# A block's row maxima, split before or after they are transposed: four 32x32 transposes on VectorE instead of one on TensorE with a rounding on ScalarE

## The chip, the cores and the metric

One core of a Trainium2 chip runs the whole kernel. The metric is the time of one execution on the device in microseconds (us). Five engines work side by side, each through its own list of instructions in order: TensorE (PE in the profile, with its weight loads as PEld), VectorE (DVE), ScalarE (ACT), GpSimd (POOL), and SyncE (SP), which here only issues the transfers (DMAs). An instruction waits on semaphores for what it needs from others, and everything behind it on its engine waits with it.

## The reference

Eight sequences of 1024 tokens with 256 features go through an attention layer with rotary positions (16 heads of 16, four shared key heads) and then a layer with ternary weights; each layer has a normalization before it, one behind it, and the residual added.

```python
q = x @ Wq; k = x @ Wk; v = x @ Wv            # x: layernorm of (8, 1024, 256)
k = jnp.repeat(k.reshape(B, S, Hkv, hd), G, axis=2)   # H = 16, Hkv = 4, G = 4, hd = 16
v = jnp.repeat(v.reshape(B, S, Hkv, hd), G, axis=2)
q = _rope(q, ...); k = _rope(k, ...)
scores = jnp.einsum('bhqd,bhkd->bhqk', q, k) / jnp.sqrt(jnp.float32(D))   # D = 256
p = jax.nn.softmax(scores, axis=-1)
o = jnp.einsum('bhqk,bhkd->bhqd', p, v)
...
x = x + _layernorm(o.reshape(B, S, D) @ Wo)
x = x + _layernorm(jnp.einsum('bsd,od->bso', _layernorm(x), ternary(weight) * alpha) + bias)
```

The part that matters here is the softmax: before the exponential, each row of scores has its largest score subtracted.

## The kernel before, in words

The work is cut into 16 units of 512 queries (half a sequence each), and a unit into 4 blocks, so there are 64 blocks. A block holds four heads of 512 queries (in the last unit: all sixteen heads of 128 queries), against the 1024 keys of its sequence. Queries and keys lie stacked in `q_st` and `k_st` with 64 rows for a head: three bands of 16 rows hold the high and low parts of the numbers (so that products in the rounded type `F32R` come out nearly exact), and rows 48 and 49 (`NROW`) are kept for the maxima: the keys have -1 there, and the queries first 0 and later the high and the low part of the query's maximum. One product then gives the score less its maximum.

So each block is gone through twice. In the first pass (`max_scores`, L583 to L619) TensorE forms the scores with queries on partitions, two half rows of 512 keys to a tile `sm` in PSUM (L600), of which there are two, and VectorE reduces each tile to its maxima in `mx` (`reduce_halves`, L625): either both halves in one instruction of 128x1024, or one half at a time (128x512), as the order has it. In the second pass (`exp_one`) TensorE forms the scores with keys on partitions in a tile `se` (L673), of which there are three, each one bank of PSUM; ScalarE takes the exponential (L694) into `e`, and TensorE multiplies by the values (`av_piece`, L714). The first pass runs 40 to 52 of these score tiles ahead of the second; a block has 32 of them.

The order on TensorE, VectorE and ScalarE is written out by hand. The loop goes by **windows** (`window`, L1164): for each of 3 score tiles (or 2) it records one `se` product with its exponential and one half row of maxima, and behind them the products with the values of the window before last. Other work that needs a bank of PSUM for itself (projections, transposes, the output layers of units before and after; `banked`, L1093) takes its bank from the three of `se`. Where such a piece of work stands ready, the window has 2 score tiles, and one piece is done in the bank that is left (`window_size`, L1105; `do_parts`, L1127). GpSimd and SyncE are ordered by the scheduler of the framework.

The change is in what happens once a block's maxima are complete:

- `shift_join` (L638) reduces the two half rows to one maximum on VectorE and writes it twice, for the high and the low part: `mc`, 128x32 from 128x64 (L642). The queries are still on partitions.
- Some steps later (`due`, L619; `collect`, L1122) `shift_rows` (L644) is put at the head of the ready work. It is `banked`: a window of 2 tiles carries it. TensorE transposes `mc` into `pm`, 32x128 in PSUM (L648), and ScalarE rounds `pm` to `F32R` into `mh` (L650).
- In the next window, `shift_low` (L653, called by `take_low`, L1140) lets VectorE compute `ml` = `mh` * `low` + `pm` (L657), where `low` is a column with -1 on the rows of the low part and 0 on the others, made at the start (L525 to L528). Rows of the high part then hold the rounded maximum, the others what rounding left. Two DMAs of SyncE (L664) write the 32 rows into rows 48 and 49 of `q_st`.

The block's first exponential product waits for these two DMAs; `behind_shift` and `behind_latest` (L1017, L1022) place some other DMAs behind them in SyncE's list.

Of the kernel before, what the change touches and what calls it, by code (L numbers as in the profile page):

```python
# [8 lines left out]
F32 = mybir.dt.float32  # L9
F32R = mybir.dt.float32r  # L10
AF = mybir.ActivationFunctionType
ALU = mybir.AluOpType
AX = mybir.AxisListType
# [3 lines left out]
P = 128  # L17
# [4 lines left out]
UT = 4  # L22
# [6 lines left out]
def kernel(  # L29
# [29 lines left out]
    nc = tc.nc  # L59
# [13 lines left out]
    const = ctx.enter_context(tc.tile_pool(name="const", bufs=1))  # L73
    xp = ctx.enter_context(tc.tile_pool(name="xp", bufs=2))
    small = ctx.enter_context(tc.tile_pool(name="small", bufs=4))
# [107 lines left out]
    def psum(shape, name, dtype=F32):  # L183
        if spare[0]:
            spare[0] += 1
            if spare[0] % 5 < 2:
                return ps_mx.tile(shape, dtype, tag="sm", name=name)
        return ps_e.tile(shape, dtype, tag="se", name=name)
# [314 lines left out]
    def row_pickers():  # L503

        sel = q_st[1].rearrange("p j c t -> p (j c t)")[:, : 4 * G * P]
        nc.vector.memset(sel.bitcast(F32), 0.0)
        sel = sel.rearrange("p (l e j x) -> p l e j x", l=2, e=2, j=G)
        selk = tailp.tile([P, 2, P], F32R, tag="hl1", name="selk")
        nc.vector.memset(selk.bitcast(F32), 0.0)
        half = small.tile([P, P // 2], F32, tag="half", name="half", bufs=1)  # L510
        nc.vector.tensor_tensor(half, ident[:, : P // 2], ident[:, P // 2 :], ALU.add)
        eye = half.rearrange("p (a j d) -> p j a d", a=2, j=G)
        for e in range(2):
            for band, l in enumerate((0, 1, 0)):
                rows = sel[:, l, e].rearrange("p j (a b d e) -> p j a b d e", a=2, e=2, d=HD // 2)
                nc.vector.tensor_copy(rows[:, :, :, band, :, e], eye)
        eye = ident.rearrange("p (l r a d) -> p l r a d", l=2, r=2, a=2)
        for band, l in enumerate((0, 0, 1)):
            rows = selk.rearrange("p r (a b d) -> p r a b d", a=2, d=HD)
            nc.vector.tensor_copy(rows[:, :, :, band, :], eye[:, l])  # L520
        shift = const.tile([P, 1], F32, name="shift")
        rows = ident.rearrange("p (a d) -> p a d", a=2)[:, :, NROW:]
        nc.vector.tensor_reduce(shift, rows, AX.XY, ALU.add)
        nc.vector.tensor_scalar(shift, shift, -1.0, None, ALU.mult)
        low = const.tile([8 * UT, 1], F32, name="low")  # L525
        rows = ident[: 8 * UT, : 8 * UT].rearrange("p (a l x) -> p a l x", a=2, l=2)[:, :, 1]
        nc.vector.tensor_reduce(low, rows, AX.XY, ALU.add)
        nc.vector.tensor_scalar(low, low, -1.0, None, ALU.mult)  # L528
        return sel, selk, shift, low

    class PickRows:

# [38 lines left out]
    mx = {}  # L571
# [11 lines left out]
    def max_scores(v):  # L583


        i, k = divmod(v // 2, 2 * NK)
        u, part = i // G, v % 2
        if i == 0:
            a, ch, t, r2 = 1 - part, k // NK, k // 2 % UT, k % 2
        else:  # L590
            a, ch, t, r2 = 1 - k % 2, part, k // 4, k // 2 % 2
        queries = block_queries(i, r2)
        queries = queries[:, t * P : (t + 1) * P] if u < NU - 1 else queries[:, t]
        if part == 0:
            sm[0] = ps_mx.tile([P, 2, 512], F32, tag="sm", name=f"sm_{i}_{k}")
            if k == 0:
                mx[i] = small.tile([P, 2, 2 * UT, 2], F32, tag="mx", name=f"mx_{i}")
            reduced.clear()
        rows = slice(64 * a, 64 * a + 64)
        scores = nc.tensor.matmul(  # L600
            sm[0][:, part, :],
            queries[rows],
            k_st[(u // UPB) % 3][rows, r2, ch * 512 : (ch + 1) * 512],
            start=True,
            stop=True,
        )
        if part == 0:
            return
        if reduced:
            tc.declare_no_dep(scores.ins, early[0], reason="another bank")  # L610
        if i == 0:
            nc.vector.tensor_reduce(
                mx[i][:, ::-1, head_and_tile(i, r2, t), ch], sm[0], AX.X, ALU.max
            )
        else:
            reduce_halves(i, k, 2)
        if k == 2 * NK - 1:
            shift_join(i)
            due.append((v // 4 + (1 if i < 3 else 2), i))  # L619

    def reduce_halves(i, k, n):

# [10 lines left out]
        if i > 0 and v % 2:  # L633
            reduce_halves(i, k, 1)

    sm, mhl, shifts, reduced, early = {}, {}, {}, [], [None]

    def shift_join(i):  # L638

        m = mhl[i] = small.tile([P, 2, 2, 2 * UT], F32, tag="mc", name=f"mc_{i}")  # L640
        halves = mx.pop(i).unsqueeze(2).to_broadcast([P, 2, 2, 2 * UT, 2])
        nc.vector.tensor_reduce(m, halves, AX.X, ALU.max)  # L642

    def shift_rows(i):  # L644

        m = mhl.pop(i)
        pm = psum([8 * UT, P], f"pm_{i}")
        nc.tensor.transpose(pm, m.rearrange("p a l x -> p (a l x)"), ident)  # L648
        mh = work.tile([8 * UT, P], F32R, tag="mh", name=f"mh_{i}")
        nc.scalar.copy(mh, pm)  # L650
        mhl[i] = pm, mh

    def shift_low(i):  # L653

        pm, mh = mhl.pop(i)
        ml = work.tile([8 * UT, P], F32R, tag="ml", name=f"ml_{i}")
        nc.vector.scalar_tensor_tensor(ml, mh.bitcast(F32), sels[3], pm, ALU.mult, ALU.add)  # L657
        n = 4 * UT
        for a in range(2):
            row = 64 * a + NROW  # L660
            dst = block_queries(i)[row : row + 2].bitcast(F32)
            if len(dst.shape) == 4:
                dst = dst.rearrange("l j c t -> l (j c) t")
            shifts[i] = nc.sync.dma_start(out=dst, in_=ml[n * a : n * a + n, :].bitcast(F32)).ins  # L664


    es, av_ps, av_sb, d_av = {}, {}, {}, {}
# [421 lines left out]
    def maxima_by(s):  # L1089

        return s + 4 * START + 2 * sum(s >= k for k in (28, 36, 52, 68, 84, 100))

    def banked(f, args):  # L1093

        return f in (shift_rows, threshold, transpose_ternary) or (
            f is part and args[2] in ("x", "xw", "q", "v", "kv_and_dram", "attn", "ffn", "n", "o")
        )

# [20 lines left out]

    def collect(n):  # L1120

        if due and due[0][0] <= maxima_by(4 * n + 4) // 4 - 1:  # L1122
            i = due.pop(0)[1]
            ready.insert(0, (shift_rows, (i,)))
        ready.extend(todo.pop(n, ()))

    def do_parts(banks):  # L1127

        while ready:
            f, args = ready[0]  # L1130
            if banked(f, args):
                if banks == 0:
                    break
                banks -= 1
            ready.pop(0)
            f(*args)
            if f is shift_rows:
                split_later.append(args[0])

    def take_low():  # L1140
        while split_later:
            shift_low(split_later.pop(0))

    def start_step(n):
        for q in range(4):
            max_scores(maxima[0])
            maxima[0] += 1
            if q == 1:
                take_low()
        collect(n)  # L1150
        do_parts(99)

    behind, done, split_later = [], [], []

    def av_windows(lag):

# [7 lines left out]
    def window(s):  # L1164


        late, size = s >= ends, window_size(s)
        if done:
            av_out(done.pop())
        if late:  # L1170
            for r2 in range(2):
                exp_two(s // 4, r2)
        else:
            end = min(maxima_by(s + size), 4 * NSTEP)
            for q in range(max(size, end - maxima[0])):
                if q < size:
                    exp_one(s + q)
                if maxima[0] < end:
                    max_scores(maxima[0])
                    maxima[0] += 1  # L1180
                if q == 0:
                    take_low()
            reduce_early(maxima[0])
        take_low()
        behind.append((s // (4 * NK), s, size))
        for n in range(s // 4, (s + size) // 4):
            collect(n)
        do_parts(3 - size if REGULAR <= s < ends else 99)
        av_windows(1 if late else 2)
        return s + size  # L1190

    E = mybir.EngineType
    due, picks = [], []
    with tc.manual_schedule(engines={E.PE, E.DVE, E.Activation, E.Pool}):
        sels = row_pickers()
        warm.append(ps_av.tile([P, UQ], F32, tag="av", name="warm"))
# [56 lines left out]
    with tc.manual_schedule(engines={E.PE, E.DVE, E.Activation}):  # L1253
        while s < 4 * NSTEP:
            s = window(s)
        av_windows(0)
        av_out(NU * G - 1)
        assert not (todo or due or ready or split_later)
    spare[0] = 1
    with tc.manual_schedule(engines={E.PE, E.DVE, E.Activation, E.Pool}):  # L1260
        last = tails[NU - 1]
# [67 lines left out]
```

## Time and profile before

| what | value |
|---|---|
| time, median of 3 runs | 1624.39 us (1623.93 to 1625.12) |
| span of the profiled execution | 1625.2 us |
| granted TensorE clock, mean | 0.997 |
| first exponential of the second pass starts | 60.5 us |
| last block's `mc` | 1568.7 us |
| ScalarE's rounding `mh` (L650) | 64 of 243 ns |
| TensorE's transpose `pm` (L648) | 64 of 284 ns, and weight loads of 94 ns |
| transfers, mean | 73 GB/s; the packets of the main queue take 29.7% of 16 engines' span |

The page gives for each engine its busy time and share of the span; then groups of instructions by source line with their count, total and mean duration, and how long the engine had been idle just before them and for whom it waited. The view of the waits sums such idle time by pairs of engines. The timeline lists instructions by their start, with equal neighbours merged, and the view by windows sums the busy time in a stretch that is given. "128x512 f32" is partitions by elements.

### The profile page before, as it was taken

The page shows a single profiled execution, that of the slowest core. Times are in us where ns is not written, and L with a number is a line of the kernel's source. Part 1 is how long each engine was busy: PE and PEld are TensorE (multiplying, and loading weights), DVE is VectorE, ACT ScalarE, POOL GpSimd, SP SyncE. Part 2 cuts the span into 40 slices and gives each one's busy share as a digit, 9 for nine tenths or more (in the row PEclk, how much of TensorE's full clock was granted, in tenths as well). Part 3 has the DMA queues.
Part 4 walks back from the last instruction along what each step waited for, and adds up shares of the span by engine and source line. Part 5 has one row for each costly group of instructions (what it writes and reads, how often), then busy time and mean ns, then how long its engine had stood idle before and what let it go on. Part 6 is the DMA issues. An engine that isn't in the chain of part 4 may idle for free.

```text
span 1625.2 us, 37184 instructions
## 1 busy us (share of the span) xinstructions
PE 1576.5 (97%) x14702; PEld 813.9 (50%) x14702; DVE 1397.1 (86%) x2046; ACT 1270.1 (78%) x2473; POOL 833.8 (51%) x1239
## 2 busy tenths in 40 slices
PE   8999999999999999999999999999999999999997
PEld 6544454454545545454554545455454554444444
DVE  7878888889898888989889898988989888999964
ACT  4667878778787887878788787887878787787774
POOL 5542365364744637455364845546474552333354
PEclk9999999999999999999999999999999999999999
DMA  4151525124151422514133151513314141131100
GB/s 140 53 88 46 113 70 96 57 77 99 57 109 47 102 63 59 120 57 97 59 83 77 57 128 39 105 54 83 79 57 97 46 107 45 42 75 34 43 15 27
DMA packets 86078, 117.98 MB, mean 73 GB/s; under 512 B 12088, under 2 KB 50808, under 8 KB 85752
## 3 DMA queue, kind: packets, MB, share of 16 engines
q1 hardware_dynamic: 85904, 115.60, 29.7%
q8 instruction: 116, 1.90, 0.5%
q14 instruction: 58, 0.48, 0.1%
HBM read 68.65 MB, written 45.88 MB: 70 GB/s over the span
## 4 chain that ended last, share of the span: by engine, by line
PE 81%; DVE 10%; POOL 3%; ACT 2%; issue 2%; DMA 1%; SPq 0%; POOLq 0%; ACTq 0%; DVEq 0%
PE av L714 29%; PE se L673 28%; PE sm L600 9%; DVE mx L625 8%; PE pa L301 3%; PE pq L301 3%; PE pf L301 2%; ACT e L694 2%; PE pt_xt L267 2%; PE pt_ot L267 1%; PE pkv L301 1%; PE pm L648 1%; DVE bnst L237 1%; POOL lnsc L242 0%; DMA x<-in_L_attn_x 0%
## 5 line engine op out<-in xcount | busy, mean ns | idle before, releaser
L625 DVE TENSOR_REDUCE mx<-sm 128x2 f32<-128x1024 f32 (+1 forms) x1301 | 1204.8, 975 | 183.6 <-PE sm L600 164.0
L694 ACT ACTIVATE e<-se 128x512 f32<-128x512 f32 x1996 | 1057.0, 603 | 220.9 <-PE sm L600 163.7
L600 PE MATMUL sm<-k_st,q_st 64*128 64x512 f32 x2048 | 746.5, 448 | 7.2 <-DVE mx L625 4.1
L673 PE MATMUL se<-q_st,k_st 64*128 64x512 f32 x2048 | 705.6, 441 | 18.4 <-ACT e L694 14.6
L714 PE MATMUL av<-e,v_aug 128*32 128x256 f32 (+3 forms) x8584 | 606.0, 378 | 0.0
L673 PEld LDWEIGHTS se<-q_st,k_st 64*128 64x128 f32 x2048 | 324.5, 184 | 396.6 <-ACT e L694 305.4
L600 PEld LDWEIGHTS sm<-k_st,q_st 64*128 64x128 f32 x2048 | 325.2, 184 | 66.4 <-DVE mx L625 44.9
L714 PEld LDWEIGHTS av<-e,v_aug 128*32 128x32 f32 x8584 | 193.5, 108 | 212.5 <-issue 148.9
L241 POOL TENSOR_SCALAR lnsc<-mv 128x2 f32<-128x2 f32 (+1 forms) x134 | 26.1, 195 | 333.1 <-DVE mv L239 326.6
L788 POOL TENSOR_TENSOR xn<-xn,a 128x512 f32<-128x512 f32 x30 | 38.4, 1282 | 135.3 <-DMA a<-d_rec 130.0
L242 POOL TENSOR_TENSOR lnsc<-lnsc,mhalf 128x2 f32<-128x2 f32 (+1 forms) x134 | 92.5, 690 | 0.9
L157 POOL TENSOR_SCALAR xs<-xn 128x512 fp32r<-128x512 f32 x27 | 16.8, 621 | 130.8 <-DMA dq<-hlq 129.5
L162 POOL TENSOR_TENSOR hl<-xn,hl 128x512 fp32r<-128x512 f32 x54 | 68.7, 1285 | 0.1
L253 POOL TENSOR_SCALAR xn<-x,lnsc 128x256 f32<-128x256 f32 x116 | 64.3, 562 | 2.3
L853 POOL TENSOR_TENSOR a<-a,bias_bc 128x512 f32<-128x512 f32 x30 | 38.4, 1279 | 51.9 <-ACT a L852 51.9
L301 PE MATMUL pa<-woh,hl 128*128 128x256 f32 x240 | 46.2, 294 | 1.1 <-ACT e L694 1.1
L237 DVE BATCH_NORM_STATS2 bnst<-x 128x6 f32<-128x256 f32 x124 | 46.0, 413 | 1.3 <-DMA x<-in_L_attn_x 1.3
L315 POOL TENSOR_TENSOR t<-q_rot,sin_q_sb 128x512 f32<-128x512 f32 x31 | 39.7, 1282 | 12.2 <-ACT q_rot L457 12.1
L237 DVE BATCH_NORM_STATS2 bnst<-a 128x6 f32<-128x256 f32 x120 | 44.5, 413 | 0.0
L301 PE MATMUL pq<-xt,wqkvh 128*128 128x256 f32 x256 | 44.1, 294 | 0.5 <-ACT e L694 0.5
L457 ACT COPY q_rot<-pq 128x512 f32<-128x512 f32 x32 | 18.7, 586 | 28.3 <-PE pq L301 28.3
L301 PEld LDWEIGHTS pa<-woh,hl 128*128 128x128 f32 x240 | 34.6, 189 | 12.1 <-issue 6.3
(164 smaller groups left out, 1333.0 us busy)
## 6 DMA issues: line engine op xcount, KB each, us to landing
q_st<-dq SPq DMA_DIRECT2D x90, 256.0 KB
dq<-hlq SPq DMA_DIRECT2D x60, 256.0 KB
d_av<-avsb SPq DMA_DIRECT2D x60, 256.0 KB
x<-in_L_attn_x SPq DMA_DIRECT2D x15, 512.0 KB
xn<-d_av SPq DMA_DIRECT2D x30, 256.0 KB
a<-d_rec SPq DMA_DIRECT2D x30, 256.0 KB
xr<-in_L_attn_x SPq DMA_DIRECT2D x15, 512.0 KB
out_x<-a SPq DMA_DIRECT2D x30, 256.0 KB
```

The lines of the kernel that those rows point to most:

```text
L162: eng.tensor_tensor(lo, src, hi.bitcast(F32), ALU.subtract)
L237: nc.vector.bn_stats(st[:, t, :], src[:, t, :])
L242: nc.gpsimd.tensor_tensor(sc[:, 1, :], sc[:, 1, :], mhalf[:, :n], ALU.pow)
L253: eng.tensor_scalar(dst[:, t, :], src[:, t, :], sc[:, 0, t : t + 1] if eng is nc.gpsimd else mv[:, t, 0:1], sc[:, 1, t : t + 1], ALU.add i ...
L267: nc.tensor.transpose(pt[:, c, t * P : (t + 1) * P], src[:, t, c * P : (c + 1) * P], ident_r)
L301: nc.tensor.matmul(out, chunk(left[i], c), chunk(right[j], c), start=(k == 0), stop=(k == len(steps) - 1),)
L315: eng.tensor_tensor(dst, x, table.unsqueeze(1).to_broadcast(list(x.shape)), ALU.mult)
L600: scores = nc.tensor.matmul(sm[0][:, part, :], queries[rows], k_st[(u // UPB) % 3][rows, r2, ch * 512 : (ch + 1) * 512], start=True, stop= ...
L625: early[0] = nc.vector.tensor_reduce(mx[i][:, a, head_and_tile(i, r2, t), lo:n], sm[0][:, lo:n, :], AX.X, ALU.max).ins
L673: nc.tensor.matmul(sc if len(queries.shape) == 2 else sc.rearrange("p (j t) -> p j t", j=G), k_st[(i // G // UPB) % 3][rows, r2, kt * P : ...
L694: nc.scalar.activation(e, sc, AF.Exp, scale=1.0 / D**0.5)
L714: nc.tensor.matmul(av_ps[0][32 * r : 32 * r + 32, lo:hi], va[:, kt, r, :], es[i * NK + kt, r // 2, r % 2][:, lo:hi], start=(kt == 0 and lo ...
```

## The change

The maxima are split into high and low part while queries are still on partitions, and the transpose goes from TensorE to VectorE. `shift_join` now does everything in one go, at the place where it stood: VectorE reduces to one maximum (128x16 from 128x32, no longer written twice), copies it with rounding into the high half of `mhl`, subtracts that from the maximum into the low half, and transposes the 128x32 result in four squares of 32x32 into `mt`, 32x128. Each square reads another group of 32 partitions and writes other columns of the same 32 partitions. The two DMAs follow from `mt`. `shift_rows`, `shift_low`, `take_low`, `due` and the column `low` are gone, and with `shift_rows` one `banked` piece of work for each block, by which the hand-written windows are sized.

```diff
     def shift_join(i):
-        m = mhl[i] = small.tile([P, 2, 2, 2 * UT], F32, tag="mc", name=f"mc_{i}")
-        halves = mx.pop(i).unsqueeze(2).to_broadcast([P, 2, 2, 2 * UT, 2])
-        nc.vector.tensor_reduce(m, halves, AX.X, ALU.max)
-    def shift_rows(i):
-        m = mhl.pop(i)
-        pm = psum([8 * UT, P], f"pm_{i}")
-        nc.tensor.transpose(pm, m.rearrange("p a l x -> p (a l x)"), ident)
-        mh = work.tile([8 * UT, P], F32R, tag="mh", name=f"mh_{i}")
-        nc.scalar.copy(mh, pm)
-        mhl[i] = pm, mh
-    def shift_low(i):
-        pm, mh = mhl.pop(i)
-        ml = work.tile([8 * UT, P], F32R, tag="ml", name=f"ml_{i}")
-        nc.vector.scalar_tensor_tensor(ml, mh.bitcast(F32), sels[3], pm, ALU.mult, ALU.add)
-        n = 4 * UT
+        n = 2 * UT
+        m = small.tile([P, 2, n], F32, tag="mc", name=f"mc_{i}")
+        nc.vector.tensor_reduce(m, mx.pop(i), AX.X, ALU.max)
+        hl = small.tile([P, 2, 2, n], F32R, tag="mhl", name=f"mhl_{i}")
+        nc.vector.tensor_copy(hl[:, :, 0], m)
+        nc.vector.tensor_tensor(hl[:, :, 1], m, hl[:, :, 0].bitcast(F32), ALU.subtract)
+        mt = small.tile([4 * n, P], F32, tag="mt", name=f"mt_{i}")
+        rows = hl.bitcast(F32).rearrange("p a l x -> p (a l x)")
+        for b in range(UT):
+            quad = slice(32 * b, 32 * b + 32)
+            nc.vector.transpose(mt[:, quad], rows[quad])
         for a in range(2):
             row = 64 * a + NROW
             dst = block_queries(i)[row : row + 2].bitcast(F32)
...
-            shifts[i] = nc.sync.dma_start(out=dst, in_=ml[n * a : n * a + n, :].bitcast(F32)).ins
+            shifts[i] = nc.sync.dma_start(out=dst, in_=mt[2 * n * a : 2 * n * (a + 1), :]).ins
...
-        return f in (shift_rows, threshold, transpose_ternary) or (
+        return f in (threshold, transpose_ternary) or (
...
     def collect(n):
-        if due and due[0][0] <= maxima_by(4 * n + 4) // 4 - 1:
-            i = due.pop(0)[1]
-            ready.insert(0, (shift_rows, (i,)))
         ready.extend(todo.pop(n, ()))
```

More of the change, by code (lines that the diff above doesn't have):

```diff
@@ L524, in row_pickers @@
         nc.vector.tensor_scalar(shift, shift, -1.0, None, ALU.mult)
[L525 to L529, printed above, removed]
+        return sel, selk, shift
     class PickRows:
@@ L618, in max_scores @@
             shift_join(i)
-            due.append((v // 4 + (1 if i < 3 else 2), i))
     def reduce_halves(i, k, n):
@@ L634, in reduce_early @@
             reduce_halves(i, k, 1)
-    sm, mhl, shifts, reduced, early = {}, {}, {}, [], [None]
+    sm, shifts, reduced, early = {}, {}, [], [None]
     def shift_join(i):
-        m = mhl[i] = small.tile([P, 2, 2, 2 * UT], F32, tag="mc", name=f"mc_{i}")
-        halves = mx.pop(i).unsqueeze(2).to_broadcast([P, 2, 2, 2 * UT, 2])
-        nc.vector.tensor_reduce(m, halves, AX.X, ALU.max)
-    def shift_rows(i):
-        m = mhl.pop(i)
-        pm = psum([8 * UT, P], f"pm_{i}")
-        nc.tensor.transpose(pm, m.rearrange("p a l x -> p (a l x)"), ident)
-        mh = work.tile([8 * UT, P], F32R, tag="mh", name=f"mh_{i}")
-        nc.scalar.copy(mh, pm)
-        mhl[i] = pm, mh
-    def shift_low(i):
-        pm, mh = mhl.pop(i)
-        ml = work.tile([8 * UT, P], F32R, tag="ml", name=f"ml_{i}")
-        nc.vector.scalar_tensor_tensor(ml, mh.bitcast(F32), sels[3], pm, ALU.mult, ALU.add)
-        n = 4 * UT
+        n = 2 * UT
[9 more added lines that the diff above has]
+            nc.vector.transpose(mt[:, quad], rows[quad])
         for a in range(2):
@@ L1136, in do_parts @@
             f(*args)
[L1137 to L1142, printed above, removed]
     def start_step(n):
@@ L1147, in start_step @@
             maxima[0] += 1
-            if q == 1:
-                take_low()
         collect(n)
         do_parts(99)
-    behind, done, split_later = [], [], []
+    behind, done = [], []
     def av_windows(lag):
@@ L1180, in window @@
                     maxima[0] += 1
-                if q == 0:
-                    take_low()
             reduce_early(maxima[0])
-        take_low()
         behind.append((s // (4 * NK), s, size))
@@ L1192 @@
     E = mybir.EngineType
-    due, picks = [], []
+    picks = []
     with tc.manual_schedule(engines={E.PE, E.DVE, E.Activation, E.Pool}):
@@ L1257 @@
         av_out(NU * G - 1)
-        assert not (todo or due or ready or split_later)
+        assert not (todo or ready)
     spare[0] = 1
```

## The prediction

> **What bounds the kernel now.** I read the page's first part, then stretches by window, then VectorE's groups, and last the waits.
>
> ```profile
> PE 1576.5 (97%) x14702; PEld 813.9 (50%) x14702; DVE 1397.1 (86%) x2046; ACT 1270.1 (78%) x2473; POOL 833.8 (51%) x1239
> ...
> PE 81%; DVE 10%; POOL 3%; ACT 2%; issue 2%; DMA 1%; SPq 0%; POOLq 0%; ACTq 0%; DVEq 0%
> ```
>
> TensorE's 97% and its 81% of the chain are not its need: ends of matmuls are modelled, and a matmul that waits behind others counts as busy. Whole windows, cut at the first exponential of each, tell more. Columns: stretch, its length, then busy time (and instructions) of each engine.
>
> ```profile
> core 0: us, PE busy (x) PEld busy (x) DVE busy (x) ACT busy (x) POOL busy (x), PEclk, DMA share, GB/s
> 675.75:686.93 11.18, 11.18 (x110) 5.06 (x107) 11.04 (x15) 9.83 (x19) 4.19 (x5) 1.00 0.32 109
> 686.93:688.60 1.67, 1.67 (x15) 0.55 (x13) 1.64 (x3) 1.21 (x4) 1.67 (x2) 1.00 0.00 0
> 688.60:690.58 1.98, 1.96 (x26) 1.08 (x24) 1.30 (x2) 1.56 (x3) 0.37 (x1) 1.00 0.01 4
> 602.14:605.21 3.07, 3.07 (x34) 2.39 (x34) 2.52 (x6) 1.67 (x3) 0.39 (x3) 1.00 0.02 5
> ```
>
> Row 1 is six windows of 3 tiles: VectorE works 11.04 of 11.18 us, ScalarE 9.83. Row 2 is the window with `pm`: 1.67 us for 2 tiles, VectorE still busy 1.64, on what it is behind with. Row 3 follows it, row 4 carries 12 products of the output layer: here VectorE idles 0.68 and 0.55 us. So VectorE sets the pace in runs of plain windows, TensorE where banked work stands in the way.
>
> ```profile
> L625 DVE TENSOR_REDUCE mx<-sm 128x2 f32<-128x1024 f32 x715 | 858.5, 1217 | 160.7 <-PE sm L600 145.8 <-PE se L673 11.9
> L625 DVE TENSOR_REDUCE mx<-sm 128x1 f32<-128x512 f32 x586 | 378.1, 680 | 22.8 <-PE sm L600 18.3 <-PE se L673 0.6
> ...
> L657 DVE SCALAR_TENSOR_TENSOR ml<-mh,low,pm 32x128 fp32r<-32x128 f32 x64 | 21.0, 328 | 3.7 <-ACT mh L650 3.7
> ...
> L642 DVE TENSOR_REDUCE mc<-mx 128x32 f32<-128x64 f32 x64 | 14.1, 220 | 2.2
> ```
>
> Back to back, 128x1024 reduces start 1.13 us apart and 128x512 ones 0.60, so three half rows take 1.73 us: the length of a plain window.
>
> **What is removed.** `pm` and `mh` go, and 61 windows of 2 tiles that carried them, 101.0 us (1.655 each). In the changed order of TensorE's instructions there are 35 more plain windows of 3 (before: 452 in 825.8 us, 1.827 each), 8 more plain ones of 2 (1.453 each) and 17 fewer windows in all. By these prices: 35 x 1.827 + 8 x 1.453 - 101.0 = -25 us. But in those 61 windows VectorE idled 3.3 us only, and its work is not removed. What can be won is idle time behind them: the windows next after `pm` idle VectorE 34.8 us, windows of the same kinds elsewhere would have 13.7 (12 with `pt_ot` at 0.40, 12 with `pt_xt` at 0.22, 34 plain at 0.10, 2 with `pa` at 1.08, 1 with `pq` at 0.73). That is 21 us. I take -21, between 0 and -25. ScalarE's 64 roundings of 0.243 us are 15.6 us on an engine that is idle 26.7 us in those windows: nothing more.
>
> VectorE loses `mc` and `ml`: 0.220 + 0.328, each overlapping its successor by 0.08 (`mc` starts at 613.28, the next reduce at 613.42): 0.39 us a block.
>
> **What is added.** Seven instructions on VectorE, one after another, between two reduces. Nearest rows, at the start of the run:
>
> ```profile
> 3.37 0.71 DVE L516 CAST q_st<-half 128x64 fp32r<-128x64 f32 x6
> ...
> 4.29 0.18 DVE L523 TENSOR_REDUCE shift<-ident 128x1 f32<-128x32 f32 x1
> 4.51 0.15 DVE L524 TENSOR_SCALAR shift<-shift 128x1 f32<-128x1 f32 x1
> ```
>
> One that needs its predecessor's result starts 0.03 after its end (4.47 to 4.51). The join: between 0.178 (this reduce) and 0.220 (old `mc`), 0.19. The rounding copy of 16 elements: between 0.15 and 0.19 (the single cast), 0.16. The subtraction: 0.15, as a 128x64 one took 0.16. With 0.03 behind each: 0.59. A 32x32 transpose stands in no row: from 0.10 (six casts in 0.71 us, one start to the next) to 0.33 (`ml`, 32x128, unoverlapped). I take 0.19, a cast's full time; four less the last overlap of 0.08 are 0.68 (0.4 to 1.3). Sum 1.27, less 0.39 removed: +0.88 us a block (+0.6 to +1.5), 56 us over 64.
>
> The Trainium skill, "VectorE: DVE Perf Modes", section "Two Vector instructions with no wait between them", has an instruction held until all earlier ones end when its input starts in another group of 32 partitions than the last one's; that speaks against this change, since squares 2 to 4 each do. No row of this trace changes groups. By it three overlaps of 0.08, some 16 us over the run, would be lost against casts that overlap.
>
> **A collision with GpSimd.** Near the end of the run VectorE subtracts and adds with both inputs in SBUF:
>
> ```profile
> 1588.31 1.28 POOL L162 TENSOR_TENSOR ot<-ot,ot 128x512 fp32r<-128x512 f32 x1
> 1588.41 1.47 DVE L823 TENSOR_TENSOR v_aug<-v_aug,xr 128x256 f32<-128x256 f32 x1
> ...
> 1590.60 0.42 DVE L908 TENSOR_TENSOR xn_last<-po,rec 128x256 f32<-128x256 f32 x1
> ...
> 1590.94 0.56 POOL L242 TENSOR_TENSOR lnsc<-lnsc,mhalf 128x1 f32<-128x1 f32 x1
> ```
>
> Beside GpSimd's wide two-input operation the 128x256 one took 1.47 us, ending 0.29 after it; beside narrow ones one of this size took 0.42. A normalization (L253) with one wide input took 1.36 in place of 0.41 at 1594.3. Old `ml` and `mc` never varied (325 to 336, 220 to 221 ns): one input came from PSUM, or there was one. The new copy and subtraction read SBUF alone. Where the subtraction would start, 0.22 us after old `mc`'s end, a wide two-input operation is running on GpSimd in 45 of 64 blocks, with 0.52 us left in the mean over all 64. If the copy waits too, followed block by block, 0.81; if neither, 0. I take 0.5, since the subtraction is of the kind that the row shows waiting: 32 us.
>
> The skill's "SBUF — State Buffer", section "Who interferes with whom", lets any GpSimd instruction that reads SBUF block a VectorE one with two SBUF inputs, and copies in a two-port mode too, until it ends. The 0.42 us beside the narrow ones doesn't show that much. By the rule in full the sum would go to 0.81 or above, by the rows to 0.5.
>
> **How much of it shows.** Added: 56 + 32 = 88 us of VectorE. In a run like row 1 all shows: of 940 score tiles in the run's middle TensorE wrote 340 within 0.1 us of VectorE's freeing the buffer. Following each block's end until VectorE next idled, 0.85 of a delay reached TensorE. From below: eleven plain windows that got a pair of statistics (0.87 us) were 0.20 to 0.25 us longer than plain ones, 0.25 of it; idle time in banked windows (some 100 us) took up the rest. I take 0.55: 48 us.
>
> Nothing else: both DMAs are now issued some 7 us sooner (`ml` starts 4.8 to 10.8 us after `mc`), and block starts had 3.1 to 10 us to spare. In SyncE's list they pass, in regular units, the load of `xr` and an output; neither is awaited soon. If that cover were gone, a transfer would be late by the 1.3 us the chain takes. The first exponential (60.5 us) hangs on 12 warming matmuls.
>
> The sum: -21 + 48 = +27 us. The profiled execution's span is 1625.2, 0.8 above the median of 1624.39; the page shows nothing around the span, so I put the difference on the median: **1652 us**.
>
> **The rivals.**
> - *No collision* (0.20): GpSimd doesn't hold 16-element operations. 56 x 0.55 - 21 = +10: 1634. For: narrow operations passed. Against: 1.47 us.
> - *VectorE is the whole bound* (0.17): copy and subtraction both wait, 0.85 shows: (56 + 52) x 0.85 - 21 = +71: 1695. For: row 1. Against: 201 us of VectorE idle between first and last exponential.
> - *The windows win* (0.13): faster. The added time falls into idle time before the next banked window, no collision, 0.25 shows: 56 x 0.25 - 25 = -11: 1613. It decides once less than 25/88, 0.28, of the added time shows. For: the statistics. Against: row 1, and 0.85.
> - That the change doesn't do what it says is out: the order has no `pm`, and 256 transposes on VectorE.
>
> **Chances.** Forecast 0.50, the rivals as given. The range, 1620 to 1690, leaves out the faster case and the far end of the second, some 0.2. A measurement tells 0.2% (3.2 us) from none: slower 0.83, same 0.04, faster 0.13.
>
> **What would show it.** Right: VectorE's busy time up by 70 to 110 us; a subtraction with a mean well above 0.2 us and a wide spread; transposes near 0.19; windows of 3 after a block's end stretched by about half a microsecond or more, with TensorE waiting for `mx`. Wrong: a subtraction always near 0.15 (first rival); idle time of VectorE down by over 60 us with a span at or below 1625 (third); transposes above 0.3, or VectorE's idle time unchanged (second).

## The result, and the profile after

The changed kernel takes 1733.38 us (median of 4 runs, 1721.28 to 1746.71) against 1624.64 us for the kernel before, run beside it: 1.067 times as long, interval 1.0615 to 1.0724. That is 109 us slower, where the prediction had 27 and its range ended at 1690.

The page's first part and chain shares, changed kernel:

```profile
span 1734.5 us, 37504 instructions
...
PE 1638.2 (94%) x14742; PEld 848.9 (49%) x14742; DVE 1480.7 (85%) x2392; ACT 1264.5 (73%) x2409; POOL 837.1 (48%) x1239
...
PE 63%; DVE 30%; issue 2%; DMA 2%; POOL 2%; ACT 1%; SPq 0%; POOLq 0%; ACTq 0%; DVEq 0%
```

VectorE's busy time rose by 83.6 us (1397.1 to 1480.7), its share of the chain from 10% to 30%. The span rose by 109.3, so more was lost than VectorE was given to do. Its groups, by shape:

```profile
L620 DVE TENSOR_REDUCE mx<-sm 128x2 f32<-128x1024 f32 x687 | 820.5, 1213 | 142.7 <-PE sm L596 114.8 <-PE se L660 22.3
L620 DVE TENSOR_REDUCE mx<-sm 128x1 f32<-128x512 f32 x642 | 417.2, 679 | 57.7 <-PE sm L596 46.8 <-PE se L660 5.0
L645 DVE STREAM_TRANSPOSE mt<-mhl 32x32 f32<-32x32 f32 x256 | 51.3, 200 | 4.8
...
L639 DVE CAST mhl<-mc 128x16 fp32r<-128x16 f32 x64 | 29.0, 453 | 2.2
...
L640 DVE TENSOR_TENSOR mhl<-mc,mhl 128x16 fp32r<-128x16 f32 x64 | 17.7, 277 | 2.2
L637 DVE TENSOR_REDUCE mc<-mx 128x16 f32<-128x32 f32 x64 | 11.9, 186 | 2.2
```

A square takes 0.200 us, never more than 0.206. The rounding copy takes 0.190 in the median but 0.453 in the mean and 1.751 at most, the subtraction 0.277 in the mean: both are held up in some blocks, as the forecast feared of the collision with GpSimd. The trace ties the holding to that engine: each of the 20 copies over 0.38 us and of the 20 subtractions over 0.25 us ended 0.01 to 0.03 us after an instruction of GpSimd did. With nothing running there, 16 copies and 32 subtractions took 0.174 to 0.178 us. Of the 20 instructions that held a subtraction 17 have one tensor input only, such as `x<-a,lnsc`. The narrow `lnsc<-lnsc,mhalf` (128x2, 0.71 us) held none of the 11 copies and 11 subtractions beside it, at 0.174 to 0.176 us.

The waits (us in total, times, longest) show who pays. The kernel before, then the changed kernel:

```profile
ACT e L694 <- PE sm L600: 163.7, 382, 3.1
...
PEld sm L600 <- DVE mx L625: 44.9, 142, 1.4
...
PE sm L600 <- DVE mx L625: 4.1, 13, 1.0
```

```profile
ACT e L681 <- PE sm L596: 243.3, 434, 4.4
...
PEld sm L596 <- DVE mx L620: 149.0, 213, 3.3
...
PE sm L596 <- DVE mx L620: 73.5, 84, 2.8
```

TensorE's waits for a free `sm` tile are the last two lines of each, up from 44.9 and 4.1 us to 149.0 and 73.5. One block's end in the timeline (start, duration, instruction, in brackets the idle time before it):

```profile
660.36 1.10 POOL L253 TENSOR_SCALAR x<-a,lnsc 128x256 f32<-128x256 f32 x2
660.65 0.19 DVE L637 TENSOR_REDUCE mc<-mx 128x16 f32<-128x32 f32 x1
...
660.87 0.22 DVE L639 CAST mhl<-mc 128x16 fp32r<-128x16 f32 x1
...
661.13 0.35 DVE L640 TENSOR_TENSOR mhl<-mc,mhl 128x16 fp32r<-128x16 f32 x1
...
661.51 0.84 DVE L645 STREAM_TRANSPOSE mt<-mhl 32x32 f32<-32x32 f32 x4
...
662.29 2.90 DVE L620 TENSOR_REDUCE mx<-sm 128x2 f32<-128x1024 f32 x3
...
663.52 0.50 PE L596 MATMUL sm<-k_st,q_st 64*128 64x512 f32 x1 [1.51 <-DVE mx L620]
...
665.37 1.08 ACT L681 ACTIVATE e<-se 128x512 f32<-128x512 f32 x2 [2.17 <-PE sm L596]
```

Here the subtraction is held: it ends at 661.48, 0.02 us after GpSimd's pair of instructions. From the join at 660.65 no reduce of a score tile starts until 662.29. Both `sm` tiles are full by then, and TensorE, whose list is in order, stands for 1.51 us at a product of the first pass; the second pass behind it stands too, and ScalarE idles 2.17 us.

One more thing appears here that the prediction had no term for: right after this stall, from 664.4 to 667.8, TensorE's granted clock is 0.5. Added up from the trace's clock records, it was at half for 12 us before and 133 us after, mostly in stretches of 3.41 us or twice that.

### The profile page after: what moved, and what is told of

It is laid out like the page before. It is cut to its first block, busy times and chain, and to the rows that moved or that the text cites. A ratio compares the mean times of both kernels' runs of the same rounds, so it can differ in the third digit from the quotient of the medians.

```text
span 1734.5 us, 37504 instructions
## 1 busy us (share of the span) xinstructions
PE 1638.2 (94%) x14742; PEld 848.9 (49%) x14742; DVE 1480.7 (85%) x2392; ACT 1264.5 (73%) x2409; POOL 837.1 (48%) x1239
## 4 chain that ended last, share of the span: by engine, by line
PE 63%; DVE 30%; issue 2%; DMA 2%; POOL 2%; ACT 1%; SPq 0%; POOLq 0%; ACTq 0%; DVEq 0%
PE av L701 22%; DVE mx L620 20%; PE se L660 19%; PE sm L596 10%; PE pq L301 3%; PE pa L301 3%; DVE mt L645 3%; DVE mhl L639 2%; DVE bnst L237 1%; PE pt_ot L267 1%; PE pkv L301 1%; DMA q_st<-dq 1%; PE pf L301 1%; DVE mhl L640 1%; PE pt_xt L267 1%
## 5 line engine op out<-in xcount | busy, mean ns | idle before, releaser
L620 DVE TENSOR_REDUCE mx<-sm 128x1 f32<-128x512 f32 (+1 forms) x1329 | 1201.8, 955 | 200.4 <-PE sm L596 161.6
L596 PE MATMUL sm<-k_st,q_st 64*128 64x512 f32 x2048 | 763.2, 456 | 79.8 <-DVE mx L620 73.5
L660 PE MATMUL se<-q_st,k_st 64*128 64x512 f32 x2048 | 720.1, 448 | 3.0 <-ACT e L691 1.4
L701 PE MATMUL av<-e,v_aug 128*32 128x256 f32 (+2 forms) x8688 | 620.2, 385 | 0.0
L660 PEld LDWEIGHTS se<-q_st,k_st 64*128 64x128 f32 x2048 | 329.8, 188 | 370.8 <-ACT e L681 255.2
L596 PEld LDWEIGHTS sm<-k_st,q_st 64*128 64x128 f32 x2048 | 329.4, 189 | 174.7 <-DVE mx L620 149.0
L701 PEld LDWEIGHTS av<-e,v_aug 128*32 128x32 f32 x8688 | 202.2, 110 | 230.2 <-issue 174.6
L645 DVE STREAM_TRANSPOSE mt<-mhl 32x32 f32<-32x32 f32 x256 | 51.3, 200 | 4.8
L301 PE MATMUL pq<-xt,wqkvh 128*128 128x256 f32 x256 | 52.5, 336 | 0.0
L301 PEld LDWEIGHTS pq<-xt,wqkvh 128*128 128x128 f32 x256 | 42.4, 230 | 11.6 <-issue 6.9
```

The source lines that it names most:

```text
L301: nc.tensor.matmul(out, chunk(left[i], c), chunk(right[j], c), start=(k == 0), stop=(k == len(steps) - 1),)
L596: scores = nc.tensor.matmul(sm[0][:, part, :], queries[rows], k_st[(u // UPB) % 3][rows, r2, ch * 512 : (ch + 1) * 512], start=True, stop= ...
L620: early[0] = nc.vector.tensor_reduce(mx[i][:, a, head_and_tile(i, r2, t), lo:n], sm[0][:, lo:n, :], AX.X, ALU.max).ins
L645: nc.vector.transpose(mt[:, quad], rows[quad])
L660: nc.tensor.matmul(sc if len(queries.shape) == 2 else sc.rearrange("p (j t) -> p j t", j=G), k_st[(i // G // UPB) % 3][rows, r2, kt * P : ...
L701: nc.tensor.matmul(av_ps[0][32 * r : 32 * r + 32, lo:hi], va[:, kt, r, :], es[i * NK + kt, r // 2, r % 2][:, lo:hi], start=(kt == 0 and lo ...
```

## The experiments

All were timed in three rounds beside the kernel before (medians there 1623.96 to 1626.31). Three theories stood at the start. A: the added VectorE time shows for a good half, and the stalls halve TensorE's clock besides. B: all of the added VectorE time shows and the clock costs nothing. C: the new windows themselves are worse.

**e1_windows_only**: the join alone; zeros are sent in place of the maxima, so copy, subtraction and squares are left out.

```diff
-        hl = ...; nc.vector.tensor_copy(...); nc.vector.tensor_tensor(...); 4 x nc.vector.transpose(...)
-            shifts[i] = nc.sync.dma_start(out=dst, in_=mt[2 * n * a : 2 * n * (a + 1), :]).ins
+            shifts[i] = nc.sync.dma_start(out=dst, in_=fill[2 * n * a : 2 * n * (a + 1), 0, :]).ins
```

> The changed kernel without the copy, the subtraction and the four transposes: each block's maxima are joined, but zeros are sent to rows 48 and 49, so nothing is subtracted from the scores. It shows what the dropped windows of 2 tiles are worth by themselves. Theory A (the added VectorE time shows for a good half, and the stalls it makes halve TensorE's clock): 1598 to 1612 us, 15 to 25 below the kernel before, clock at 0.99 or above. Theory B (all of VectorE's added time shows one to one, the clock costs nothing): the same. Theory C (the other windows are themselves worse): 1624 us or more.

1601.35 us, ratio 0.9846 (0.9811 to 0.9881): 23 us faster than before. C is out. The six instructions that were left out cost the other 132 us, with 102.7 us of VectorE's busy time (1378.0 here). The trace is of its fastest execution (1593.03 us, clock 0.999, 4 us at half clock); the other three, at 0.992 to 0.995, had more of it.

**e2_spread**: the same seven instructions; the six behind the join stand one by one behind the next six reduces.

```diff
+        later.append(copy); later.append(subtract); later.extend(squares)
 def reduce_halves(...):
         reduced.extend(range(lo, n))
+        if later:
+            later.pop(0)()
```

> The changed kernel with the same seven instructions for each block, but only the join directly at the block's end; copy, subtraction and each transpose stand behind one of the next six reduces. VectorE's work is the same to within a few us. Theory A: no stall is long enough to halve TensorE's clock; half-clock time falls from 131 to under 40 us, and the time to 1655 to 1690 us. Theory B: the work is the same, so 1715 to 1745 us whatever the clock does. Theory C: as theory B.

1659.86 us, ratio 1.0213 (1.0182 to 1.0244): 73 us less than the changed kernel for nearly the same busy time of VectorE (1471.0), with half clock at 31 us: A's range and A's sign. So B's "all of it, wherever it stands" fails; how the work lies decides.

**e3_warm**: six products without use behind a block's end, to keep TensorE's clock up while it waits. **e5_junk_alone**, run later, puts the same six into e1_windows_only.

```diff
+        sc = ahead[s + 1] = ps_e.tile([P, 512], F32, tag="se", ...)
+        for _ in range(6):
+            nc.tensor.matmul(sc, ident_r, k_st[...][:, 0, :512], start=True, stop=True)
```

> The changed kernel with six more products for each block on TensorE, written into a score tile that is overwritten next, at the place where TensorE stands waiting for VectorE behind a block's end. VectorE's chain is unchanged. Theory A: the clock stays up (half-clock time under 60 us, granted clock above 0.98) and about half of the half-clock time that goes is won: 1675 to 1705 us. Theory B: 1720 to 1750 us, whatever the clock does. Theory C: as theory B.

> e1_windows_only (copy, subtraction and squares left out) with the six products of e3_warm put in at the same place of every block; their results go nowhere. It says what the six products cost by themselves, so that e3_warm can be read. Theory A (the half clock costs about 0.45 us of run for each us of half clock, some 50 of the 109 us that the change added): the products must have cost e3_warm what the clock gave back, so here they cost 40 to 60 us over e1_windows_only, 1640 to 1660. Theory B (the clock costs nothing, the chain all): the products are free, as they were meant to be, 1600 to 1610, and the whole 132 us between this and e3_warm is the chain at full clock.

e3_warm: 1733.63 us, ratio 1.0664 (1.0631 to 1.0697), half clock down to 23 us. By itself this looks like B: no half clock, no gain. But e5_junk_alone takes 1710.12, ratio 1.0518 (1.0499 to 1.0538): the six products cost 109 us where there is no stall to hide them, more than either theory had. e3_warm traded one loss for another and can't price the clock.

**e4_windows_kept**: the transpose on TensorE and the rounding on ScalarE put back beside the change, their result not used.

```diff
+        pm = psum([8 * UT, P], f"pm_{i}")
+        nc.tensor.transpose(pm, old.pop(i), ident)
+        nc.scalar.copy(work.tile([8 * UT, P], F32R, tag="mh", ...), pm)
```

> The changed kernel with the banked piece put back for each block: TensorE transposes and ScalarE rounds as before, with results that nobody reads, so the windows have the sizes of the kernel before; VectorE's chain is that of the change. Theory A and theory B: the gain of the windows is lost, 1735 to 1760 us. Theory C (the new windows do harm): 1715 us or less.

1744.68 us, ratio 1.0773 (1.07 to 1.0847): 11 us more than the changed kernel, as A and B had it, and far above C's range. It doesn't price the windows by itself: its chains, from the join's start to the last square's end, also came out longer, 2.01 us in the mean against 1.86.

Next, place against length. D: a piece of 1.4 us or more between two reduces does the harm wherever it stands. F: the block's end is the wrong place. **e6_chain_later** puts the six in one piece behind the fourth reduce after the join.

```diff
+        later.extend([lambda: None] * 3 + [chain])
```

> The same seven instructions; the six behind the join stand in one piece, but behind the fourth reduce after it instead of right behind the block's end. Theory D (one piece is the harm: 1.4 us or more of VectorE between two reduces is longer than TensorE's two score tiles and ScalarE's queue last, wherever it stands): within 20 us of the changed kernel, 1715 to 1755. Theory F (the place is the harm: at a block's end the products of the next block and the exponentials have no reserve, a few reduces later they have): near e2_spread, 1645 to 1680.

1671.74 us, ratio 1.0277 (1.0248 to 1.0306): F's range. A few reduces later there is reserve; the very same piece costs 62 us less, and half clock is 57 us.

**e7_no_collision**: chain and place of the change, but copy and subtraction are two more reduces; the remainder is left out.

```diff
-        nc.vector.tensor_copy(hl[:, :, 0], m)
-        nc.vector.tensor_tensor(hl[:, :, 1], m, hl[:, :, 0].bitcast(F32), ALU.subtract)
+        nc.vector.tensor_reduce(hl[:, :, 0], mx[i], AX.X, ALU.max)
+        nc.vector.tensor_reduce(hl[:, :, 1], mx.pop(i), AX.X, ALU.max)
```

> The chain of the change at its place and nearly its length, but copy and subtraction are two more reduces of the maxima (about 0.19 us each, as the join), which have one input with fewer ports to share; the low part holds the rounded maximum, not the remainder. If the mean waits of the copy (0.28 us) and of the subtraction (0.10) beside GpSimd matter as they stand in the trace, 0.38 us a block go: theory D (in one piece every microsecond shows, and a bit more): 24 to 30 us less, 1700 to 1710, with less half clock perhaps 1680. If collisions fell into time that was lost anyway: within 8 us of the changed kernel.

1656.13 us, ratio 1.0196 (1.0159 to 1.0233): 77 us less, three times what was expected, for 34.1 us less of VectorE's busy time. The reason stands in the trace: the reduces never vary (175 to 178 ns), every chain takes 1.25 us to the last square's end, and between the first and last few blocks no half clock is left. Windows of one kind of block (third of a unit, from its 13th to its 29th exponential; columns as in the prediction) tell the rest. First the changed kernel, three such blocks with the same chain, 1.70 to 1.71 us; then e7_no_collision:

```profile
660.38:675.21 14.83, 13.32 (x132) 8.01 (x132) 12.20 (x24) 9.33 (x20) 11.49 (x18) 0.88 0.31 87
764.28:777.63 13.35, 11.86 (x132) 6.87 (x132) 12.09 (x24) 9.33 (x19) 9.25 (x14) 1.00 0.29 81
864.35:879.21 14.86, 13.35 (x132) 8.20 (x132) 12.09 (x24) 9.32 (x19) 11.55 (x18) 0.89 0.34 89
```

```profile
726.81:739.71 12.90, 11.85 (x132) 6.88 (x132) 11.71 (x24) 9.33 (x20) 9.37 (x15) 1.00 0.32 86
```

Rows 1 to 3 have the same number of instructions on TensorE and on VectorE. Row 2 kept its clock and is 1.5 us shorter than rows 1 and 3, which ran one stretch of 3.41 us at half. Against e7_no_collision row 2 is 0.45 us longer, and its chain 0.46 longer. So a microsecond of chain costs a microsecond, and a half-clock stretch 1.5 more (0.44 for each us of it). The same difference stands between blocks of one kind in e4_windows_kept: 15.81 against 14.28 with a chain of 2.46 to 2.48 in both.

This made theory G: length costs 0.7 to 1.0, and a chain beyond some 1.7 us (in the changed kernel no shorter one was followed by half clock from the fifth block on) costs the clock too. Rival H: length alone, the collision harming in another way. **e9_chain_plus1** and **e10_chain_plus3** lengthen e7_no_collision's chain by squares that nobody reads.

```diff
+        for b in range(1):      # e10: range(3)
+            quad = slice(32 * b, 32 * b + 32)
+            nc.vector.transpose(spare_t[:, quad], rows[quad])
```

> e7_no_collision with one more square behind the four (its result goes nowhere): the chain behind a block's end is 0.21 us longer without any part of it depending on GpSimd, about 1.46 us from the join's start. In the changed kernel no block whose chain was 1.69 us or shorter showed half clock. Theory G (two prices: each us of chain shows at 0.7 to 1.0, and a chain beyond some 1.7 us stalls TensorE so long that its clock is halved for 3.4 us, 1.5 us lost each time): no half clock inside the run's middle, 9 to 14 us more than e7_no_collision, 1664 to 1672. Rival H (the collision with GpSimd does harm in another way than by the length of the chain; length shows at about 0.7): the same here.

> e7_no_collision with three more squares: about 1.89 us from the join's start in every block, as long as the changed kernel's mean chain, with no collision in it. Theory G: half clock in the blocks of most kinds, 25 to 50 stretches of 3.4 us, so 1656 + 28 to 40 for the length + 40 to 75 for the clock: 1725 to 1770. Rival H: length alone, 1656 + 28 to 40: 1684 to 1696, clock 0.99.

e9: 1662.25 us, ratio 1.0225 (1.0192 to 1.0258), half clock 28 us, nearly as in e7 (29), but three stretches of it now lie in the run's middle, where G had none. e10: 1720.53, ratio 1.0562 (1.0521 to 1.0603), half clock 106 us: 64 us more than e7 for 0.66 us a block of work that isn't held by GpSimd. That is 4 us below G's range and 25 above H's. H is out: a chain with no collision in it costs the clock too, so the collision needs no other harm than length and clock. The medians by kind of block (blocks 13 to 50 of the 64, same stretch, us; "half" with half clock) show both prices. The chain is measured from the join's start to the last square's end:

| kernel (chain) | 1st of a unit | 2nd | 3rd | 4th |
|---|---|---|---|---|
| e1 (join only) | 10.19 | 12.72 | 11.85 | 11.84 |
| e7 (1.25 us) | 11.02 | 13.63 | 12.90 | 12.89 |
| e9 (1.48) | 11.25 | 13.84 | 13.14 | 13.02 |
| e10 (1.91) | half 12.80 | 14.28 | 13.55 | 13.56 |
| changed (1.48 to 3.5) | 11.25 | 13.96, half 16.96 | 13.35 (one block), half 14.86 | 13.93, half 15.44 |

From e7 to e10 the last three kinds grow by 0.65 to 0.67 us for 0.66 us of chain. But G was wrong on where the clock falls: in e10 it halves in every first block, where the longest time from one product's start to the next was 1.11 us, and in no third one, with 2.1 us (blocks 13 to 50). So the length of the stall alone doesn't decide (see the last section).

**e11_one_transpose**: the four squares as one instruction over 128x32, each square staying on its 32 partitions, with eight DMAs instead of two.

```diff
-        for b in range(UT):
-            quad = slice(32 * b, 32 * b + 32)
-            nc.vector.transpose(mt[:, quad], rows[quad])
+        nc.vector.transpose(mt, rows)        # mt is 128x32
```

> The changed kernel with its four squares done by one instruction of 128x32 (0.20 us in e8_gpsimd_split), at the same place; copy and subtraction stay, and can collide. Each square stays on its 32 partitions, so eight DMAs instead of two. The chain is 0.64 us shorter: 1.23 us in the mean from the join's start in place of 1.87. Theory G: few chains reach 1.7 us (only those with a collision beyond 0.8), half clock below 40 us, and 0.64 x 0.7 to 1.0 x 62 = 28 to 40 us for the length: 1640 to 1665. Theory H: 1733 less 28 to 40, 1693 to 1705. The DMAs leave earlier than in e8_gpsimd_split by some 5 us, so TensorE should wait for them in few blocks.

1667.35 us, ratio 1.0257 (1.0227 to 1.0286), half clock 42 us: 66 us less than the changed kernel, 2 us above G's range and far below H's. The chain is 1.37 us in the mean against 1.86, 0.49 less rather than 0.64, since copy and subtraction were held differently here.

**e8_gpsimd_split**, a first candidate: copy and subtraction on GpSimd, that one transpose behind the sixth reduce, eight DMAs.

```diff
+        nc.gpsimd.tensor_copy(hl[:, :, 0], m)
+        nc.gpsimd.tensor_tensor(hl[:, :, 1], m, hl[:, :, 0].bitcast(F32), ALU.subtract)
+        later.extend([lambda: None] * 5 + [squares])
```

> A candidate to beat both. Copy and subtraction on GpSimd; the four squares as one instruction of 128x32 on VectorE, behind the sixth reduce after the join; each square leaves from its own 32 partitions, so eight DMAs a block instead of two. VectorE has the join and one transpose of 0.2 us more than e1_windows_only has. Theory D: nothing of a microsecond stands between two reduces, so 0.22 us a block show to a half: 1601 + 7 = 1603 to 1618, and half clock as little as in e1_windows_only. Rivals: the transpose waits for GpSimd's queue and holds VectorE there, or the eight DMAs land too late for the block's first exponential: above 1624, with VectorE idle before the transpose or TensorE waiting for a DMA.

1716.26 us, ratio 1.0556 (1.0528 to 1.0584), the rival's case. First VectorE's transpose, then from the waits TensorE's for the DMAs:

```profile
L647 DVE STREAM_TRANSPOSE mt<-mhl 128x32 f32<-128x32 f32 x64 | 13.0, 204 | 11.7 <-POOL mhl L642 11.7
```

```profile
PE se L677 <- DMA q_st<-mt: 58.7, 25, 5.8
```

All four squares take 0.204 us in one instruction, and VectorE has only 1394.5 us to do. But eight issues of 0.61 us on SyncE, begun some 7 us after the join, land after the next block's first exponential product is due: 58.7 us of waiting in 25 blocks, and half clock for 131 us.

**e12_high_only**, a second candidate. The join writes the maxima rounded, and the remainder is left out: a shift common to all keys of a query falls out of the softmax. One transpose, four DMAs of 16 rows.

```diff
+        nc.vector.tensor_reduce(hl.rearrange("p l a x -> p a l x"), halves, AX.X, ALU.max)
+        nc.vector.transpose(mt, hl.bitcast(F32).rearrange("p l a x -> p (l a x)"))
+        for b in range(UT):
+            shifts[i] = nc.sync.dma_start(out=dst[:, :, quad], in_=mt[32 * b : 32 * b + 2 * n, :]).ins
```

> A candidate to beat both. The join writes the maxima rounded, in one instruction, and the remainder is left out: the shift in the exponent is the rounded maximum, the same for every key of a query, and falls out of the quotient. One 128x32 transpose behind it, four DMAs of 16 rows. VectorE has 0.25 us a block more than e1_windows_only, no wait beside GpSimd. Theory G: 0.25 x 0.7 x 64 = 11 us over e1_windows_only, clock as there: 1605 to 1618. Rival: four DMAs for two are late on SyncE's queue: above 1624.

1602.76 us, ratio 0.9857 (0.9836 to 0.9879): faster than both kernels, 1.4% below the one before, and 2 us below the expected range. Its two groups at the block's end, and the page's first part:

```profile
L638 DVE TENSOR_REDUCE mhl<-mx 128x32 fp32r<-128x64 f32 x64 | 14.1, 220 | 2.2
L640 DVE STREAM_TRANSPOSE mt<-mhl 128x32 f32<-128x32 f32 x64 | 13.5, 212 | 2.2
```

```profile
span 1601.0 us, 37376 instructions
...
PE 1567.6 (98%) x14742; PEld 819.1 (51%) x14742; DVE 1392.3 (87%) x2072; ACT 1258.8 (79%) x2409; POOL 837.0 (52%) x1239
```

The whole chain is 0.47 us, VectorE has 4.8 us less to do than before, half clock is 8 us, and the gain of the windows is kept.

## Why the prediction was wrong

The step that failed is **How much of it shows**: "I take 0.55: 48 us." Set against e1_windows_only, the added work was 102.7 us of VectorE and cost 132: 1.29, not 0.55. The 109 us divide as follows.

| part | us | from |
|---|---|---|
| windows without `pm`, smaller join | -23 | e1 against before |
| chain of 1.25 us at the block's end, nothing colliding | +55 | e7 against e1, 0.80 of 68.6 us |
| longer chain through collisions | +24 to +34 | copy 0.28 and subtraction 0.10 us over e7's, 64 blocks; or all the busy time that VectorE has over e7, at 1.0 |
| 105 us more at half clock than in e7 | +46 | 0.44 for each us |
| sum | 102 to 112 | measured 109 |

The first three rows hold some half clock themselves, as it differs from execution to execution. The mean granted clock of each execution is on record, and with it the time at half clock. Among the executions of one kernel (73 in all, of the changed kernel, the experiments and the kernel before) each us more at half went with 0.45 us more of span (0.24 to 0.67 in single kernels), the price that the blocks had shown. An estimate takes half clock out at that price, by the medians of 3 us before, 16 in e1, 27 in e7 and 122 in the changed kernel: the first three rows become -28, +50 and +35, and the clock +53. So at full clock the added work showed to 0.82 (85 of 102.7 us). With that share the prediction's own sum would have come to 1676, inside its range; the clock, for which its "Nothing else" left no term, takes the time out of it.

Two things went wrong in that step. The share was taken over the run's mean, and from pairs of statistics of 0.87 us that stand where VectorE has reserve. A chain in one piece behind a block's end has little: two `sm` tiles fill, and at full clock 0.73 of a clean chain shows (50 of 68.6 us), and about all of what is beyond it. Spread (e2: 59 of 93 us) or four reduces later (e6: 70 of 94) less of it shows, at full clock 51 and 48 us. That is the prediction's 0.55: it fits a place with reserve, and this place has little. The other part, the clock, had no place in the sum at all. The profile of before, at 0.997 with 12 us of half clock, held hardly an instance of it, but the prediction went only as far as TensorE waiting for `mx`, without asking what a stalled TensorE costs when it goes on.

Step by step:

- *Windows, -21.* About right. e1 gained 23 (28 at full clock), though it also took 19.1 us off VectorE, so the windows alone gave rather less.
- *VectorE's added time, +88.* Measured +83.6; that it came so near is in part luck, since two misses offset each other. The join (0.186 for 0.19) was right. Collisions were sized 0.12 us a block too high, and squares 0.17 too low: they take 0.200 and start 0.213 apart, with no overlap, where casts at the run's start began 0.10 apart. The Trainium skill, "VectorE: DVE Perf Modes", section "Two Vector instructions with no wait between them", had that against the change; the rows agree with it for the squares.
- *Collision, 0.5 us a block.* 0.38, the mechanism as told, but copies were held as well as subtractions, the case for which the prediction had 0.81. Its row for narrow operations that pass, `xn_last<-po,rec` at 0.42 us, doesn't have both inputs in SBUF: `po` lies in PSUM (L894). So it showed nothing of them; the 22 rows beside `lnsc` above do. The price of the collision was missed: 77 us between e7 and the changed kernel instead of 18, because it lengthened a chain all of whose excess shows, and the half clock came with it.
- *DMAs cost nothing.* Right with two of them; e8 shows the cover gone.
- *Rivals.* "No collision" was tried as e7: 1656 where 1634 was worked out, low again by the share. "VectorE is the whole bound" had the better share (0.85) and still ended 38 us short, without the clock. "The windows win" needed a share below 0.28, and no run had one; e12 wins with the same windows because it adds no time to VectorE.
- *The signs.* Busy time up by 70 to 110, a subtraction well above 0.2 with spread, squares near 0.19, TensorE waiting for `mx`: all came. The stretch behind a block's end grew by far more than the half microsecond named: from the 17th to the 21st exponential of a block, where the stall falls, it is 5.41 us in place of 3.16 in e1 (means of blocks 13 to 50), 2.2 more.

What stays open: collisions beyond copy and subtraction (the 10 us between the two figures of the third row), and the first three blocks, which ran long stretches at half clock in e10 and in the changed kernel; they are in the clock's row at the price of the middle.

## What to carry to other kernels

Price a chain of small instructions by what stands behind it in the one place where it is put: how long the buffers last there, and what the next engine does once it has run dry. A short stall of TensorE can cost much more than its length: here one of 1.9 us was followed by 3.4 us at half clock, which cost another 1.5, or by none, as it lay. Cut such a chain before moving it: one instruction over 128 partitions did four squares for the price of one, and half of what was transposed, the remainders, wasn't needed.

## What the runs showed of the hardware

- The half clock comes on a grid. In the changed kernel its stretches from 248 us on, but for the last, are 3.41 us or 6.83 long, and all their starts lie on one grid of 3.413 us to within 0.01. Where a stall lies on the grid matters as well as its length. In the three blocks of the changed kernel shown under e7_no_collision TensorE stalled for 1.89 to 1.90 us. Two of these stalls lay mostly or wholly in a single step, and half clock followed; the border at 766.82 us cut the third into 1.30 and 0.59 us, and none followed.
- As a measure of activity I take each product from its start to the next one's, at most 0.23 us. TensorE then filled 0.42 and 0.37 of the two steps, and 0.60 and 0.69 of the two that share the third stall. By this count each of the 21 stretches between 248 and 1600 us follows a step filled to 0.46 or less, and of the other 350 full-clock steps three lie below 0.49. In e10 the two groups overlap, from 0.43 to 0.54, and another cap than 0.23 us moves the limit: at 0.4 us the steps before a stretch reach 0.61, and 0.74 in e10. So where the limit lies, and in what measure, stays open. That e10 was hit in every first block and in no third one fits the grid too: its half-clock stretches there come 102.4 us apart, thirty steps, so each unit lies on the grid as the one before did, and a border cuts the third blocks' stalls of 2.1 us. The share filled hardly tells the two apart, 0.53 to 0.54 in the steps that were followed by half clock and 0.49 to 0.52 in the others.
- The Trainium skill, "TensorE: Matmul & The Clock Gate", section "Part 1: The HAM clock gate", has this free-running window of 3413 ns, and the runs agree. Its table drops the clock after an idle window of about 3.4 us; here stalls of 1.1 us (first blocks of e10) and of 1.4 us and more within a step (changed kernel) were enough, and the measurement decides.
- A 128x32 transpose on VectorE takes 0.204 to 0.212 us, a 32x32 one 0.200: four squares side by side cost what one does.
- A rounding copy of 16 elements for each partition took up to 1.75 us on VectorE beside GpSimd; a reduce in its place (e7, 128x16 from 128x32, writing the same rounded tile) took 175 to 178 ns in every block.
